# Second mixture of experts: results are scattered with addition onto stored features, and one array is read back

## The chip, the cores and the metric

The kernel runs on one core of a Trainium2 chip. Five engines matter: TensorE (PE in the profile, with its weight loads as PEld), VectorE (DVE), ScalarE (ACT), GpSimd (POOL) and SyncE (SP), which here only issues transfers. Each has its own instruction queue and waits on semaphores for the others. Sixteen DMA engines move data between the on-chip memory and the device memory; they take transfers from queues that SP, ACT and POOL fill. The metric is device time in microseconds (us) of one execution.

## The reference

The program is a net of four layers on a graph of N = 2708 nodes with D = 256 features, all in 32-bit floats. Each layer adds to the features x what a graph attention gives, and then what a feed-forward part gives. The change lies in the feed-forward part of layer 2, a decoder block with a mixture of experts:

```
x    = x + attention(rmsnorm(x)) @ wo.T          # causal, 4 heads
flat = rmsnorm(x)
probs = softmax(flat @ router_w.T)               # 8 experts
tp, ti = top_k(probs, 2)
tp   = tp / (sum(tp) + 1e-9)                     # the two shares of a node
weights = sum(tp[..., None] * one_hot(ti, 8))
for e in range(8):
    hh  = silu(flat @ w1[e].T) * (flat @ w3[e].T)    # 682 hidden units
    out = out + weights[:, e] * (hh @ w2[e].T)
x    = x + out
```

So each node's result is its own x, after attention, plus two weighted expert results. Layer 3 begins by normalizing that x and projecting it for its graph attention.

## The kernel before, in words

The features x stay on chip in an array X of 22 tiles of 128 nodes (the last has 20). `net_kernel` (L2406) runs the layers in order; `decoder_ffn` (L1486) is layer 2's feed-forward part and `elu_gnn` (L2368) layer 3's attention.

**Attention (L1878).** Nodes go in chunks of 512 (five, and a rest of 148). For each chunk `send` (L2052) multiplies by wo on PE, adds to X on POOL (L2066), forms the normalized row h and the logits of the eight experts, and then runs `Routing.chunk` (L1632). The order of PE is written out by hand: the score and value products run in groups of two steps, and between them one piece of the generator `sends`, up to its next `yield`, is let in (two pieces a group in the last column). The last chunk's `send` runs inside the mixture. On the other engines a planner sets the order by the data's dependences and by the `issue_after` marks.

**Routing (`Routing`, L1556).** `chunk` finds each node's two best experts, counts nodes per expert, ranks each node within its expert by two small PE products (L1661, L1662), and so gives each of its two choices a slot. Per tile of nodes, two indirect transfers on POOL (L1682) scatter the rows of h to the array hs in device memory, which is ordered by slots. A row carries 256 features and two tags (L1680): the node's number and the slot of its first choice.

**Mixture (`experts`, L2184).** `through` (L2266) runs over 47 slot tiles of 128 rows, each of one expert. For a tile it loads f from hs, transposes it (`front`), multiplies by w1 and w3 (`hidden`, L2226), applies silu on ACT, multiplies on DVE (`gate`, L2243), transposes again (L2250, copied to ht by DVE at L2251 and ACT at L2252), multiplies by w2 (`results`, L2258) and copies y out of PSUM on ACT (L2262). There are three buffers of y and two of hh, whose padding POOL clears (L2237). `where` (L1818) finds each row's target with three small DVE operations, and `send` (L1831) scatters y by an indirect transfer on POOL (L1834) to `ys`, which has one block of rows for first choices, one for second choices, and spare rows for empty slots. All targets are distinct, which line L1841 declares, so a send waits for no other send.

The queue of SP carries the loads of the weights: w2 early, w1 (L1552) from 1829.5 us, w3 from 1890.7 us, then the loads of f.

**Weights and end.** After the last slot tile's silu and gate, `shares` (L1501, called at L2355) computes the softmax over all logits and the two shares of every node, for all tiles together. `combine` (L1846) then reads both blocks of `ys` back, on the queues of SP, POOL and ACT, and `gat_single` (L1301), layer 3's attention, draws on it chunk by chunk: four tiles get their eight weighted additions on DVE (L1872), then the norm (L160 to L167, L124), the transposes (L1346) and projections on PE. Layer 1's top-1 mixture uses the same class with one choice: one array, one addition a tile. After the reads, the graph's mask is loaded again (L2452).

Of the kernel before, what the change touches and what calls it, by code (L numbers as in the profile page):

```python
# [8 lines left out]
F32 = mybir.dt.float32  # L9
# [3 lines left out]
ALU = mybir.AluOpType  # L13
# [1472 lines left out]
def decoder_ffn(net, ctx):  # L1486

    nc, tc, a = net.nc, net.tc, net.a  # L1490
    big = ctx.enter_context(tc.tile_pool(name="d_big", bufs=1))
    dram = ctx.enter_context(tc.tile_pool(name="d_dram", bufs=1, space=bass.MemoryType.DRAM))
    route = Routing(net, big, dram, 2, "d")
    ln2 = net.load_rows(big, a["d_ln2"], D, "ln2")
    router = net.load_weight(big, a["d_routerT"], "router")
    prep = ctx.enter_context(tc.tile_pool(name="g3prep", bufs=1))
    with ExitStack() as inner:
        weights = Weights(net, inner)
        heads = []

        def shares(work):  # L1501

            route.weights(work)
            total = work.tile([P, NT], F32, name="total")
            nc.vector.tensor_tensor(total, route.weight[:, 0, :], route.weight[:, 1, :], ALU.add)
            nc.vector.tensor_scalar(total, total, 1e-9, None, ALU.add)
            nc.vector.reciprocal(total, total)
            for c in range(2):
                nc.vector.tensor_tensor(route.weight[:, c, :], route.weight[:, c, :], total, ALU.mult)

        def head(work=None):

            if work is None:
                for _ in heads[0].fold():
                    pass
            else:
                heads.append(Head(net, prep, work, "g3", False))

        def mixture(after, rest):
            experts(net, route, weights, after, rest, head, shares)  # L1520

        attention(net, route, ln2, router, weights, mixture)
    return heads[0], route
# [32 lines left out]
class Routing:  # L1556
# [10 lines left out]
    def __init__(self, net, pool, dram, choices, key):  # L1567
# [4 lines left out]
        if choices == 1:  # L1572

            self.hs = dram.tile([E * CAP, 1], F32, name=f"{key}nodes")
        self.ys = dram.tile([(choices * NT + self.tiles) * P, D], F32, name=f"{key}ys")
        self.logits = pool.tile([P, NT, E], F32, name=f"{key}logits")
# [3 lines left out]

        self.tag = pool.tile([P, NT, 2], F32, name=f"{key}tag")
        nc.gpsimd.iota(
# [19 lines left out]
        for t, pattern, base, step in (  # L1602
            (self.s, [[1, S]], -E, 0),
            (self.at, [[0, 1]], 0, 1),
            (self.place, [[P, S]], choices * NT * P, 1),
        ):
            nc.gpsimd.iota(t, pattern, base=base, channel_multiplier=step, allow_small_or_imprecise_dtypes=True)
# [4 lines left out]
        if choices == 1:  # L1612
            zero = pool.tile([P, E * CAP // P], F32, name=f"{key}zero")
            nc.vector.memset(zero, 0.0)
            nc.scalar.dma_start(self.hs.rearrange("(p c) d -> p (c d)", p=P), zero)
        self.expert = pool.tile([1, S], I32, name=f"{key}expert")
        self.further = pool.tile([1, 1], I32, name=f"{key}further")
# [14 lines left out]
    def chunk(self, work, psum, t0, n, source, tag="pr"):  # L1632
# [3 lines left out]
        key = self.key  # L1636
        rest = self.logits[:, t0 : t0 + n, :]
        for c in range(self.choices):
            one, _ = first_max(nc, work, rest, net.rev, (n, E), P, f"{key}f{c}")
            oc = self.one[:, c, t0 : t0 + n, :]  # L1640
# [16 lines left out]
        nc.vector.tensor_copy(self.count, so_far[:, n, :])  # L1657
        yield
        ps = psum.tile([P, n, E], F32, name="rank", tag=tag)
        flat = ps.rearrange("p n e -> p (n e)")  # L1660
# [13 lines left out]
        for k in range(n):  # L1674
# [6 lines left out]
            for c in range(self.choices):  # L1681
# [7 lines left out]
                tc.declare_no_dep(i.ins, group=f"{key}scatter", reason="slots are distinct")  # L1689
                tc.add_to_no_dep_group(f"{key}scatter", i.ins)  # L1690

    def cut(self, psum, tag):
# [125 lines left out]
    def where(self, work, s, f, cut=False):  # L1818

        nc = self.net.nc  # L1820
        own, taken, spare = self.cuts if cut else (self.own, self.taken, self.spare)
        to = work.tile([P, 1], I32, name="to", bufs=8)
        at = work.tile([P, 1], F32, name="second", bufs=3)
        nc.vector.tensor_scalar(
            at, f[:, D + 1 :], own[:, s : s + 1], float(NT * P), ALU.not_equal, ALU.mult
        )
        nc.vector.tensor_scalar(at, at, f[:, D : D + 1], taken[:, s : s + 1], ALU.add, ALU.mult)
        nc.vector.tensor_tensor(to, at, spare[:, s : s + 1], ALU.add)
        return to

    def send(self, to, y):  # L1831
# [46 lines left out]
def attention(net, route, ln2, router, weights, mixture):  # L1878
# [11 lines left out]
    with ExitStack() as ctx:  # L1890
# [161 lines left out]
        def send(n, rp, aux, tag="aux"):  # L2052
# [6 lines left out]
            for k, t in enumerate(its):  # L2059
# [6 lines left out]
                nc.gpsimd.tensor_tensor(X[:r, t, :], X[:r, t, :], xa[:r], ALU.add)  # L2066
                h = hs[t] = rp.tile([P, D + 2], F32, name="h", bufs=len(its) + 1)
# [115 lines left out]

def experts(net, route, weights, after, rest, head, shares):  # L2184

# [6 lines left out]
    with ExitStack() as ctx:  # L2192
# [7 lines left out]
        def fetch(s, engine=None):  # L2200
            fs[s] = work.tile([P, D + 2], F32, name="f", bufs=E)
            route.load(s, fs[s], engine)
# [52 lines left out]
        def results(s, ht):  # L2255
# [5 lines left out]
            y = work.tile([P, D], F32, name="y", bufs=3)  # L2261
            nc.scalar.copy(y, po)  # L2262
            route.send(tos.pop(s), y)
            return last
# [65 lines left out]
        def routing():  # L2330
# [13 lines left out]
            with tc.issue_after(copied[-1].ins), tc.issue_after(route.sent.ins):  # L2344
                head(room)
            rooms.append(room)

        rooms, silus, gates, copied = [], [], [], []
        with tc.issue_after(after.ins):
# [56 lines left out]
def net_kernel(ctx, tc, a, out):  # L2406
# [3 lines left out]
    kept = dram.tile([N, N], U8, name="kept")  # L2410
    net.hs = dram.tile([Routing.E * CAP, D + 2], F32, name="hs")
    with ExitStack() as graph:
# [16 lines left out]
def clear_dispatch(net, pool):  # L2429

    nc = net.nc
    zero = pool.tile([P, D + 2], F32, name="zero")
    nc.gpsimd.memset(zero, 0.0)
    for e in range(Routing.E):
        nc.sync.dma_start(
            net.hs[e * CAP : (e + 1) * CAP].rearrange("(t p) d -> p t d", p=P),
            zero.unsqueeze(1).to_broadcast([P, NT, D + 2]),
        )
# [112 lines left out]
```

## Time and profile before

Three runs took 2600.6, 2603.6 and 2616.84 us. The table is of the profiled execution.

| what | value |
|---|---|
| median of the runs | 2603.6 us |
| the profiled execution's own time | 2609.1 us |
| its span | 2607.2 us |
| mean granted PE clock | 0.967 |
| attention of layer 2, last chunks | 1560 to 1895 us |
| PE's wait for the first f of the mixture | ends at 1904.96 us |
| last send of the mixture | 2301.21 us |
| first transpose of layer 3 | 2320.78 us |
| first attention product of layer 3 | 2366.31 us |

Times are read as microseconds from the start of the span. A line of a timeline gives the start, the duration, the engine, the line of the kernel, the operation with its output and inputs, the number of instructions put together, and in brackets how long the engine had been idle and what released it. A "q" after an engine's name is its instruction queue, in which it issues transfers.

### The profile page before, as it was taken

Reading aid. Unit: us, or ns where it says so; the run is one execution under the profiler, and the core shown is the slowest. Engines: PE = TensorE matmul, PEld = TensorE weight load, DVE = VectorE, ACT = ScalarE, POOL = GpSimd, SP = SyncE. Lnnn points to the kernel's source line nnn. Section 1 sums busy time; section 2 is a strip of 40 time slices with the busy share of each in tenths; the row PEclk is TensorE's granted clock in tenths of the full one; section 3 lists DMA queues with packets and bytes.
Section 4 is the critical chain, followed back from the end, with each engine's and each line's share of the span. In section 5 each row is a group of like instructions: output and inputs, shape, how many; then the busy total and the mean of one; then the engine's idle time right before and its main releaser. Section 6 shows DMA issues by size and latency. Waiting matters only on the chain. (4 is left out here: it accounts for less than half of the span.)

```text
span 2607.2 us, 32662 instructions
## 1 busy us (share of the span) xinstructions
PE 2422.9 (93%) x11708; PEld 1574.6 (60%) x11708; DVE 1477.6 (57%) x3288; ACT 1051.7 (40%) x1692; POOL 336.2 (13%) x476
## 2 busy tenths in 40 slices
PE   5899998999999998979799989999979999969998
PEld 4666765685333334568588854444457777747886
DVE  7754437746888875333545458778742222264556
ACT  3444443214787762321444324344412222234454
POOL 1000003100000000144130011222321111110002
PEclk9999999979999999989899999999989999979999
DMA  8899611000000003774310010000341111050001
GB/s 289 285 291 317 200 57 62 1 6 1 1 1 1 1 1 103 174 186 136 96 58 1 1 39 9 19 17 17 113 142 33 33 33 33 19 206 6 1 1 43
DMA packets 106859, 197.58 MB, mean 76 GB/s; under 512 B 8862, under 2 KB 63752, under 8 KB 103860
## 3 DMA queue, kind: packets, MB, share of 16 engines
q1 hardware_dynamic: 88010, 146.82, 18.2%
q0 software_dynamic: 14880, 43.76, 5.2%
q10 hardware_dynamic: 3806, 4.85, 0.6%
q8 instruction: 99, 1.62, 0.3%
q14 instruction: 64, 0.52, 0.1%
HBM read 135.69 MB, written 59.71 MB: 75 GB/s over the span
## 5 line engine op out<-in xcount | busy, mean ns | idle before, releaser
L732 DVE SCALAR_TENSOR_TENSOR e<-e,mask 128x768 f32<-128x768 f32 (+3 forms) x352 | 417.5, 1217 | 242.0 <-ACT e L731 239.4
L731 ACT ACTIVATE e<-big_p,minus_one,ratio 128x768 f32<-128x768 f32 (+3 forms) x352 | 418.6, 1226 | 281.3 <-PE acc L1463 193.4
L1463 PE MATMUL acc<-V,e 128*128 128x257 f32 x1848 | 401.9, 380 | 5.7 <-DVE e L732 5.6
L1463 PEld LDWEIGHTS acc<-V,e 128*128 128x128 f32 x1848 | 350.3, 190 | 57.5 <-issue 7.0
L2226 PE MATMUL h<-w,ft 128*128 (+1 forms) x752 | 234.5, 453 | 0.5 <-ACT ft L2208 0.5
L307 PE MATMUL acc<-F,e 128*128 128x257 f32 (+1 forms) x924 | 212.5, 383 | 4.1 <-DVE e L303 3.8
L928 PE MATMUL acc<-e,V 128*64 128x512 f32 (+1 forms) x1056 | 208.6, 547 | 1.3 <-DVE e L732 1.3
L307 PEld LDWEIGHTS acc<-F,e 128*128 128x128 f32 (+1 forms) x924 | 171.6, 189 | 57.0 <-DVE e L303 29.6
L2243 DVE TENSOR_TENSOR hh<-hh,h 128x682 f32<-128x682 f32 x47 | 40.7, 866 | 243.6 <-PE h L2226 243.6
L2226 PEld LDWEIGHTS h<-w,ft 128*128 128x128 f32 x752 | 135.9, 191 | 56.5 <-issue 1.8
L928 PEld LDWEIGHTS acc<-e,V 128*64 128x64 f32 x1056 | 73.6, 137 | 150.7 <-issue 145.6
L2014 ACT ACTIVATE e<-sc 128x1024 f32<-128x1024 f32 (+4 forms) x131 | 107.5, 863 | 137.5 <-PE sc L2005 97.8
L303 DVE TENSOR_TENSOR e<-e,mask 128x512 f32<-128x512 f32 (+2 forms) x132 | 80.5, 621 | 140.4 <-ACT e L296 138.7
L2036 DVE TENSOR_TENSOR sum<-sum,e 128x1024 f32<-128x1024 f32 (+4 forms) x131 | 137.1, 1047 | 20.6 <-PE po L2030 7.4
L296 ACT ACTIVATE e<-score 128x512 f32<-128x512 f32 (+2 forms) x132 | 69.4, 544 | 171.0 <-PE score L294 145.9
L2258 PE MATMUL po<-w,ht 114*128 (+1 forms) x564 | 131.5, 383 | 0.9 <-DVE ht L2251 0.9
L2005 PE MATMUL sc<-qt,kt 64*128 64x512 f32 (+5 forms) x568 | 121.0, 544 | 1.1 <-ACT sum L2014 0.9
L2258 PEld LDWEIGHTS po<-w,ht 114*128 114x128 f32 x564 | 107.6, 191 | 23.1 <-DVE ht L2251 8.2
L939 PE MATMUL den<-e,low 128*3 128x512 f32 (+1 forms) x1056 | 117.7, 542 | 0.0
L294 PE MATMUL score<-QK 128*128 128x512 f32 (+2 forms) x264 | 112.1, 553 | 3.4 <-ACT e L296 3.0
L2030 PE MATMUL po<-e,V 128*64 128x512 f32 (+5 forms) x524 | 108.5, 531 | 1.9 <-DVE e L2020 1.5
L2252 ACT COPY ht<-pt 114x256 f32<-114x256 f32 x47 | 17.5, 372 | 200.7 <-DVE ht L2251 200.7
(647 smaller groups left out, 3381.1 us busy)
## 6 DMA issues: line engine op xcount, KB each, us to landing
row<-in_adj SPq DMA_DIRECT2D x21, 1354.0 KB
raw<-in_adjT SPq DMA_DIRECT2D x35, 768.0 KB
hs<-zero SPq DMA_DIRECT2D x8, 2838.0 KB
hidden<-hr SPq DMA_DIRECT2D x32, 256.0 KB
wd<-in_f_wd SPq DMA_DIRECT2D x8, 1024.0 KB
kept<-mask SPq DMA_DIRECT2D x21, 338.5 KB
mask<-kept SPq DMA_DIRECT2D x21, 338.5 KB
w<-in_d_w1T SPq DMA_DIRECT2D x8, 682.0 KB
```

Source lines behind the costliest of these rows:

```text
L294: nc.tensor.matmul(ps[:r, :iw], QK[:, 0, span(j)], QK[:, 1, i0 : i0 + iw], start=True, stop=True)
L307: ended = nc.tensor.matmul(acc[k], e[:r, k * P : (k + 1) * P], F[:r, j, :], start=j == 0, stop=j == NT - 1)
L731: nc.scalar.activation(v, big_p[:, i], AF.Relu, bias=net.minus_one, scale=ratio)
L732: return nc.vector.scalar_tensor_tensor(v, v, 1.0, net.mask[:, j, i], ALU.add, ALU.mult)
L928: nc.tensor.matmul(acc[n][half, :iw], V[:, j, h, :], e[n][:, k, :iw], start=j == 0, stop=j == NT - 1)
L939: nc.tensor.matmul(den[g : g + Q, :iw], low[:, j, h, Q - 1 - q : 2 * Q - 1 - q], e[n][:, k, :iw], start=False, stop=j == NT - 1 and q == Q ...
L1463: nc.tensor.matmul(acc[k][:ri], e[:, k * P : k * P + ri], V[:, j, :], start=j == 0, stop=j == NT - 1)
L2005: nc.tensor.matmul(by_pairs(ps[:r, g], m, iw)[:, :, o:], kt[b, span(j)], qt[b, :, o:iw], start=True, stop=True)
L2030: nc.tensor.matmul(by_pairs(outs[n, p][b], m, iw)[:, :, o:], V[:r, j, g, :], by_pairs(e[:r, g], m, iw)[:, :, o:], start=j == 0, stop=j == ...
L2036: nc.vector.tensor_tensor(total, total, by_heads(e[:r], m, iw)[:, :, :, o:], ALU.add)
L2226: last = nc.tensor.matmul(halves[s, n][:, q, :HALF], fts[s][:, c, :], weights.w13[n][:, es[s], c, q * HALF : (q + 1) * HALF], start=c == 0 ...
L2258: last = nc.tensor.matmul(po, ht[:KP, k, :], w2[:KP, es[s], k, :], start=k == 0, stop=k == KC - 1)
```

## The change

For the mixture with two choices:

- `chunk` computes the shares of its nodes itself (the new `Routing.shares`: ten DVE operations and one Exp on ACT for each chunk, and one more `yield`). They travel as two more tags with h, so that a row of hs has 260 floats and not 258. The softmax after the last slot tile is gone.
- `send` of the attention stores the new X of its chunk to `ys` (`keep`, seven transfers on SP's queue in all). `ys` has one block of node rows, and one block of spare rows that is zeroed at the start.
- `where` takes four small DVE operations: one for the target, three for the row's own share. The copy of y on ACT multiplies by that share.
- The scatter of y adds to what its target row holds (`compute_op` add). Two sends can have rows in common, so the declaration that they are independent is left out, and a send waits for the one before.
- `combine` reads the one array straight into X by nine transfers on SP's queue. The weighted additions on DVE are gone.
- `left` does for slot tiles beyond the usual 47 what `where` had done with a bigger spare block; it runs only if there are such tiles.

The mixture with one choice keeps its path, with a tag array of four columns.

```diff
@@ Routing.__init__
-        self.ys = dram.tile([(choices * NT + self.tiles) * P, D], F32, name=f"{key}ys")
+        spare = self.tiles if choices == 1 else 1
+        self.ys = dram.tile([(NT + spare) * P, D], F32, name=f"{key}ys")
...
-        self.tag = pool.tile([P, NT, 2], F32, name=f"{key}tag")
+        self.tag = pool.tile([P, NT, 4], F32, name=f"{key}tag")
...
+        else:
+            zero = pool.tile([P, D], F32, name=f"{key}zero")
+            nc.vector.memset(zero, 0.0)
+            nc.scalar.dma_start(self.ys[NT * P :, :], zero)
@@ Routing.chunk
         nc.vector.tensor_copy(self.count, so_far[:, n, :])
         yield
+        if self.choices == 2:
+            self.shares(work, t0, n, *most)
+            yield
         ps = psum.tile([P, n, E], F32, name="rank", tag=tag)
@@ new in Routing
+    def shares(self, work, t0, n, top, second):
+        nc, E, key = self.net.nc, self.E, self.key
+        e = work.tile([P, n, E + 1], F32, name=f"{key}e")
+        nc.vector.tensor_tensor(
+            e[:, :, :E], self.logits[:, t0 : t0 + n, :], top.unsqueeze(2).to_broadcast([P, n, E]), ALU.subtract
+        )
+        nc.vector.tensor_tensor(e[:, :, E], second, top, ALU.subtract)
+        nc.scalar.activation(e, e, AF.Exp)
+        w0, w1 = self.tag[:, t0 : t0 + n, 2], self.tag[:, t0 : t0 + n, 3]
+        nc.vector.tensor_reduce(w0, e[:, :, :E], AX.X, ALU.add)
+        nc.vector.reciprocal(w0, w0)
+        nc.vector.tensor_tensor(w1, e[:, :, E], w0, ALU.mult)
+        total = work.tile([P, n], F32, name=f"{key}sum")
+        nc.vector.scalar_tensor_tensor(total, w0, 1e-9, w1, ALU.add, ALU.add)
+        nc.vector.reciprocal(total, total)
+        for w in (w0, w1):
+            nc.vector.tensor_tensor(w, w, total, ALU.mult)
+
+    def keep(self, its):
+        for k0, k1, r in whole_and_rest(its):
+            r0 = its[k0] * P
+            self.net.nc.sync.dma_start(
+                self.ys[r0 : r0 + (k1 - k0 - 1) * P + r, :].rearrange("(t p) d -> p t d", p=r),
+                self.net.X[:r, its[k0] : its[k0] + k1 - k0, :],
+            )
@@ Routing.where
         to = work.tile([P, 1], I32, name="to", bufs=8)
-        at = work.tile([P, 1], F32, name="second", bufs=3)
-        nc.vector.tensor_scalar(
-            at, f[:, D + 1 :], own[:, s : s + 1], float(NT * P), ALU.not_equal, ALU.mult
-        )
-        nc.vector.tensor_scalar(at, at, f[:, D : D + 1], taken[:, s : s + 1], ALU.add, ALU.mult)
-        nc.vector.tensor_tensor(to, at, spare[:, s : s + 1], ALU.add)
-        return to
+        w = work.tile([P, 2], F32, name="share", bufs=8)
+        slot = f[:, D + 1 : D + 2]
+        nc.vector.scalar_tensor_tensor(to, f[:, D : D + 1], taken, spare, ALU.mult, ALU.add)
+        nc.vector.tensor_scalar(w[:, 1:], slot, own, f[:, D + 3 :], ALU.not_equal, ALU.mult)
+        nc.vector.tensor_scalar(w[:, :1], slot, own, f[:, D + 2 : D + 3], ALU.is_equal, ALU.mult)
+        nc.vector.tensor_tensor(w[:, :1], w[:, :1], w[:, 1:], ALU.add)
+        return to, w[:, :1]
@@ Routing.send
             in_offset=None,
+            **({} if self.choices == 1 else {"compute_op": ALU.add}),
         )
-        tc.declare_no_dep(i.ins, group=f"{self.key}results", reason="rows are distinct")
-        tc.add_to_no_dep_group(f"{self.key}results", i.ins)
+        if self.choices == 1:
+            tc.declare_no_dep(i.ins, group=f"{self.key}results", reason="rows are distinct")
+            tc.add_to_no_dep_group(f"{self.key}results", i.ins)
@@ Routing.combine
+        if self.choices == 2:
+            for t0, t1 in ((0, 1), (1, 2), (2, 4), (4, 8), (8, 12), (12, 16), (16, 20), (20, NT)):
+                for k0, k1, r in whole_and_rest(range(t0, t1)):
+                    r0 = (t0 + k0) * P
+                    self.read = nc.sync.dma_start(
+                        X[:r, t0 + k0 : t0 + k1, :],
+                        self.ys[r0 : r0 + (k1 - k0 - 1) * P + r, :].rearrange("(t p) d -> p t d", p=r),
+                    )
+            yield
+            return
@@ attention.send
+            route.keep(its)
             for k, t in enumerate(its):
@@ experts.results
             y = work.tile([P, D], F32, name="y", bufs=3)
-            nc.scalar.copy(y, po)
-            route.send(tos.pop(s), y)
+            to, share = tos.pop(s)
+            nc.scalar.activation(y, po, AF.Copy, scale=share)
+            route.send(to, y)
@@ experts, end
-        with tc.issue_after(silus[-1].ins), tc.issue_after(gates[-1].ins):
-            shares(rooms[0])
         with route.others():
+            route.left()
             through(0, E)
             through(route.usual, route.tiles)
```

More of the change, by code (lines that the diff above doesn't have):

```diff
@@ L1499, in decoder_ffn @@
         heads = []
[L1501 to L1509, printed above, removed]
         def head(work=None):
@@ L1519, in mixture @@
         def mixture(after, rest):
-            experts(net, route, weights, after, rest, head, shares)
+            experts(net, route, weights, after, rest, head)
         attention(net, route, ln2, router, weights, mixture)
@@ L1604, in __init__ @@
             (self.at, [[0, 1]], 0, 1),
-            (self.place, [[P, S]], choices * NT * P, 1),
+            (self.place, [[P if choices == 1 else 0, S]], NT * P, 1),
         ):
@@ L1636, in chunk @@
         key = self.key
-        rest = self.logits[:, t0 : t0 + n, :]
+        rest, most = self.logits[:, t0 : t0 + n, :], []
         for c in range(self.choices):
-            one, _ = first_max(nc, work, rest, net.rev, (n, E), P, f"{key}f{c}")
+            one, top = first_max(nc, work, rest, net.rev, (n, E), P, f"{key}f{c}")
+            most.append(top)
             oc = self.one[:, c, t0 : t0 + n, :]
@@ L1690, in chunk, with left @@
                 tc.add_to_no_dep_group(f"{key}scatter", i.ins)
+    def shares(self, work, t0, n, top, second):
[22 more added lines that the diff above has]
+            )
+    def left(self):
+        nc, E, (_, done, _) = self.net.nc, self.E, self.cuts
+        taken, spare, place = self.taken[:, :E], self.spare[:, :E], self.place[:, :E]
+        nc.vector.tensor_tensor(taken, taken, done, ALU.subtract)
+        nc.vector.tensor_tensor(spare, taken, place, ALU.mult)
+        nc.vector.tensor_tensor(spare, place, spare, ALU.subtract)
     def cut(self, psum, tag):
@@ L1820, in where @@
         nc = self.net.nc
-        own, taken, spare = self.cuts if cut else (self.own, self.taken, self.spare)
+        own, taken, spare = (t[:, s : s + 1] for t in (self.cuts if cut else (self.own, self.taken, self.spare)))
         to = work.tile([P, 1], I32, name="to", bufs=8)
-        at = work.tile([P, 1], F32, name="second", bufs=3)
-        nc.vector.tensor_scalar(
-            at, f[:, D + 1 :], own[:, s : s + 1], float(NT * P), ALU.not_equal, ALU.mult
-        )
-        nc.vector.tensor_scalar(at, at, f[:, D : D + 1], taken[:, s : s + 1], ALU.add, ALU.mult)
-        nc.vector.tensor_tensor(to, at, spare[:, s : s + 1], ALU.add)
-        return to
+        w = work.tile([P, 2], F32, name="share", bufs=8)
[5 more added lines that the diff above has]
+        return to, w[:, :1]
     def send(self, to, y):
@@ L2066, in send @@
                 nc.gpsimd.tensor_tensor(X[:r, t, :], X[:r, t, :], xa[:r], ALU.add)
-                h = hs[t] = rp.tile([P, D + 2], F32, name="h", bufs=len(its) + 1)
+                h = hs[t] = rp.tile([P, D + 4], F32, name="h", bufs=len(its) + 1)
                 nc.scalar.activation(h[:r, :D], xa[:r], AF.Square, accum_out=ss[:r, k : k + 1])
@@ L2181, in whole_and_rest, with experts @@
     return [(0, n, P)] + [(k, k + 1, rows(its[k])) for k in range(n, len(its))]
-def experts(net, route, weights, after, rest, head, shares):
+def experts(net, route, weights, after, rest, head):
     nc, tc = net.nc, net.tc
@@ L2200, in fetch @@
         def fetch(s, engine=None):
-            fs[s] = work.tile([P, D + 2], F32, name="f", bufs=E)
+            fs[s] = work.tile([P, D + 4], F32, name="f", bufs=E)
             route.load(s, fs[s], engine)
@@ L2345, in routing @@
                 head(room)
-            rooms.append(room)
-        rooms, silus, gates, copied = [], [], [], []
+        silus, gates, copied = [], [], []
         with tc.issue_after(after.ins):
@@ L2410, in net_kernel @@
     kept = dram.tile([N, N], U8, name="kept")
-    net.hs = dram.tile([Routing.E * CAP, D + 2], F32, name="hs")
+    net.hs = dram.tile([Routing.E * CAP, D + 4], F32, name="hs")
     with ExitStack() as graph:
@@ L2431, in clear_dispatch @@
     nc = net.nc
-    zero = pool.tile([P, D + 2], F32, name="zero")
+    zero = pool.tile([P, D + 4], F32, name="zero")
     nc.gpsimd.memset(zero, 0.0)
@@ L2436, in clear_dispatch @@
             net.hs[e * CAP : (e + 1) * CAP].rearrange("(t p) d -> p t d", p=P),
-            zero.unsqueeze(1).to_broadcast([P, NT, D + 2]),
+            zero.unsqueeze(1).to_broadcast([P, NT, D + 4]),
         )
```

## The prediction, made before the changed kernel was run

> **What bounds the kernel now.** First the busy table of the page, for the engine that carries the time. In every fence below a number after an x is a count, and a figure in brackets is idle time of the engine just before, with what ended it.
>
> ```profile
> PE 2422.9 (93%) x11708; PEld 1574.6 (60%) x11708; DVE 1477.6 (57%) x3288; ACT 1051.7 (40%) x1692; POOL 336.2 (13%) x476
> ```
>
> TensorE (PE) is busy 93% of the span, so an edit on DVE, POOL or a DMA queue counts only where PE waits for it. Second, the windows of the stages that the change touches: second attention, passage into the mixture, mixture, passage to the next layer. The columns are start:end and length, then busy time of PE, PEld, DVE, ACT and POOL, the granted PE clock, the DMA share and GB/s.
>
> ```profile
> 1560.00:1850.00 290.00, 282.41 (x1314) 120.91 (x1316) 230.50 (x467) 118.05 (x167) 66.33 (x61) 0.99 0.11 39
> 1850.00:1900.00 50.00, 36.49 (x230) 19.52 (x229) 35.12 (x97) 16.80 (x34) 14.57 (x17) 0.90 0.21 75
> 1950.00:2300.00 350.00, 347.86 (x1529) 255.61 (x1528) 96.94 (x235) 75.55 (x170) 46.16 (x85) 1.00 0.11 32
> 2300.00:2312.00 12.00, 0.53 (x3) 0.12 (x1) 0.40 (x4) 1.86 (x3) 6.02 (x9) 0.64 0.37 116
> 2312.00:2345.00 33.00, 21.71 (x83) 16.07 (x84) 32.48 (x110) 15.46 (x65) 3.32 (x4) 0.77 0.99 354
> ```
>
> Attention and mixture are PE bound (97% and 99%). PE stands still in two places: the passage in (13.5 of 50 us) and the passage out. There, from 2312 on, DVE is full (32.5 of 33 us) and so is the DMA (0.99). Third, the timeline of the passage out, for what follows what (start, duration, engine, line):
>
> ```profile
> 2301.21 0.97 POOL L1834 DMA_INDIRECT dys<-y,to  x1 [8.62 <-ACT y L2262]
> ...
> 2306.64 11.69 SPq L1860 DMA_DIRECT2D y<-dys  x7
> ...
> 2311.95 3.26 DVE L1872 SCALAR_TENSOR_TENSOR X<-y,dweight,X 128x256 f32<-128x256 f32 x8 [9.27 <-DMA y<-dys]
> ...
> 2316.87 3.23 DVE L1872 SCALAR_TENSOR_TENSOR X<-y,dweight,X 128x256 f32<-128x256 f32 x8
> 2316.99 0.30 ACT L163 ACTIVATE sd<-mv,ln_eps 128x4 f32<-128x4 f32 x1 [13.72 <-DVE mv L161]
> 2320.01 0.17 DVE L167 RECIPROCAL rstd<-sd 128x4 f32<-128x4 f32 x1
> ...
> 2320.78 1.51 PE L1346 MATMUL tp<-ident,f 128*128 128x128 f32 x6 [20.25 <-DVE f L124]
> ```
>
> The last send starts at 2301.21; its landing releases the reads 5.4 us later; they deliver 5.3 us later; eight weighted additions (3.26 us) precede the norm of the first four tiles, eight more (3.23 us) fall between the square root and its reciprocal; PE starts after 20.25 us of idleness. Fourth, the passage in, and one steady period of the mixture:
>
> ```profile
> 1880.96 0.99 POOL L1682 DMA_INDIRECT hs<-h,dto  x1 [14.61 <-DVE h L1680]
> 1904.96 0.66 PE L132 MATMUL tp<-ident,f 128*128 128x128 f32 x2 [14.07 <-DMA f<-hs]
> 2103.65 0.98 POOL L1834 DMA_INDIRECT dys<-y,to  x1 [4.26 <-ACT ft L2208]
> 2106.92 0.16 DVE L1828 TENSOR_TENSOR to<-second,dspare 128x1 int32<-128x1 f32 x1
> 2107.42 0.69 DVE L2251 COPY ht<-pt 114x512 f32<-114x512 f32 x1 [0.34 <-PE pt L2250]
> 2111.81 0.98 POOL L1834 DMA_INDIRECT dys<-y,to  x1 [4.26 <-ACT ft L2208]
> ```
>
> PE's 14.07 us wait at the entry is the routing of node chunk 4 (DVE), eight scatters of h, their landing, the load of f. In the mixture sends leave every 8.15 us.
>
> **The change, part by part.** The sums are against the profiled execution: span 2607.2 us, its own time 2609.1, which is 5.5 us above the median of 2603.6; a saving is carried to the median as it stands.
>
> *Passage out.* Removed: 44 weighted additions of about 0.41 us (3.26/8) and half of the reads (two arrays of 2.77 MB become one, read into X on SP's queue alone). Step by step: (1) The last landing. The bytes of a plain send have moved about 2 us after its start (the DMA share in the middle of the mixture peaks from 1.4 to 1.9 us after 2111.81), but the waiter is released at 5.4 us here, and at 2.5 us after the last send of layer 1's mixture (1253.89, reads issued 1256.43). No row shows an adding send. It also reads each row before it writes it. Nothing can make it shorter than a plain one, which the same writes already need, but its release could fall near layer 1's 2.5 us; at worst the read costs what a small read costs (a 129 KB load of f in mid-run: issue 2123.32, bytes in by 2125, 1.7 us) plus a second write-like burst, +2.8. I take +1.5, nearer the read's row: 2301.21 + 5.4 + 1.5 = 2308.1. Here the Trainium skill helps with one term: "Collectives: The Full Stack", section "The bandwidth ceiling: the fold count and why AG ≠ RS ≠ AR", says that an add needs two source reads and so half a copy's rate. On the 0.5 us burst that is +0.5 alone; I stay at 1.5, since the trace's own landing is 3 us longer than its burst. (2) Tiles 0 to 3 arrive. Before, 1 MB took 5.3 us; half of it at the window's 354 GB/s saves 1.5 us: 3.8. From the f load's 1.7 us and 384 KB more at that rate: 2.8. I take 3.4: 2311.5. (3) With no additions, what remains is the statistics of the last two tiles to arrive (0.74 + 0.18 us), square root 0.30, reciprocal to first transpose 0.77 (2320.01 to 2320.78): 2.1 with gaps. PE starts at 2313.6 instead of 2320.78: **−7.2**. (4) The first block of four tiles took 11.35 us (2320.78 to 2332.1) against 6.5 for later ones, DVE and clock both being behind; layer 1's passage, with half the additions, took 10.35. I take −1.5, bounds 0 and −4. After that PE is the bound. Total **−8.7**, from −5 (landing +2.8, delivery 3.8) to −14 (landing 2.5 to 4).
>
> *The end softmax* (some 5 us of DVE, an Exp and its table load of 1.28 us) lay at 2291 to 2299 beside the last results on PE, before the last send: removing it is 0.
>
> *Weights by chunk.* Per chunk ten small DVE operations and an Exp. A small DVE row here is 0.16 to 0.27 us; with a pitch of 0.21, 2.1 us a chunk. Chunks 0 to 3 fall into the attention, where DVE has 59 us free of 290 but its additions are one step from PE's tail work; PE is what is full, and cover holds except where PE waits for the rank or an X tile. 0 to 8.4 us; I take +0.5, by the 97%. Chunk 4 stands in the entry chain: +2.1 for DVE, an Exp that may queue behind one of 1.22 us on ACT, and the rank matmuls come a group later in PE's written order: +0.5 to +5, taken **+2.5**. The last chunk's Exp falls into the mixture and swaps ACT's table twice (2.56 us) in gaps of over 4 us: 0, at worst +2.6.
>
> *Storing X.* Seven writes (2.77 MB) on SP behind POOL's X additions, ahead of w1 and w3 and, for the last rows, of the f loads. The first would be queued by about 1830, when w1 went out at 1829.5 before; w1 is first needed at 1906, w3 shares the wire with the f loads: 2.77 MB at 400 GB/s is 7 us over 340 us. 0; if a late X addition holds SP, w1 moves and has 70 us of slack. POOL's first send now waits for all seven and for the zero fill: the last is out some 10 us before the first y.
>
> *In the loop.* Four small DVE operations for three per slot tile (47 tiles). DVE idles 0.34 us before the copy of ht, which PE waits for; one more row of 0.16 to 0.25 fits. If not, 47 × 0.2 = +9. Evicting y with a scale: 0.47 us (the 128x256 scaled copy on ACT elsewhere in this trace) for 0.37, with over 4 us idle before: 0, and +0.1 at the end.
>
> *The chain of sends.* The plain sends of one array were independent. Now each waits on POOL for the landing of the one before. Queued behind a waiting send on POOL is the memset of a later hh (L2237), for which DVE's gate and then PE wait; ACT waits when the three y buffers are full. By the rows a landing takes 5.4 + 1.5 = 6.9 us of the 8.15: 1.25 to spare, no cost. The rule that speaks against the change is in "DMA: Bandwidth & Descriptors", section "Rules for kernel authors": an adding DMA beside another access of the same bytes loses writes, so the earlier semaphore must be waited for; hence the chain is required. Its fit in "Anatomy of one DMA — SWDGE (gpsimd) path" (2.0 us and the bytes at 436 GB/s) would make an adding send 2.3 to 2.6 us, with 5.5 to spare and an end 4 us earlier. The trace's 5.4 decides.
>
> Sum: −8.7 + 2.5 + 0.5 = −5.7: profiled 2603.4, median **2598** (2603.6 − 5.7). About 1% (26 us) is what a measurement of this kernel can tell from no change, and the whole idle time at the passage out is 20 us.
>
> **The rivals.**
> A, the forecast, 2592 to 2610: 0.61.
> B, a larger gain: the last landing is seen after 2.5 us, the chunk-4 chain hides its ten operations, and the first block runs at the full clock. The landing saves another 4.4 (6.9 − 2.5), the block 4 in place of 1.5, the entry costs 0: −7.2 −4.4 −4 gives about 2588. For it: layer 1's landing. Against it: this mixture's own 5.4. 0.14.
> C, the loss ahead of the mixture: X additions, rank and Exp in the hand-written order hold PE in each chunk, +5 at the entry and 2 in each of four chunks, with the fourth operation of the loop hit: −8.7 + 13 + 6 gives about 2614. For it: DVE 80% full. Against: PE 97% busy there. 0.11.
> D, the other side: the chain of sends becomes the bound. It decides when start to landing of an adding send passes 8.15 us, the period. A send of 128 rows is 8 rows for each of 16 engines. If an engine finishes one row's read and write before the next, at about 0.8 us a row (an estimate, from the least HBM round trip on "DMA: Bandwidth & Descriptors", section "Latency and other measured facts"; no run here shows it), it is 2.5 + 6.4 = 8.9 us, and the y buffers hand the excess to PE: 46 × 0.75 = 35, about 2633; from the base of 5.4 it would be above 2700. For it: a margin of only 1.25 us. Against: a plain send's rows overlap (0.5 us burst), and nothing says that adding stops that. 0.14.
>
> **How the numbers follow.** A's 2592 to 2610 is wide by landing, delivery and entry. The range 2585 to 2622 takes in A, most of B and C, and leaves out D and the edges, under 2 in 10. Faster by over 1% (below 2577.6) needs all of the 20 us and more: 0.04. Slower by over 1% (above 2629.6) is most of D: 0.13. Else 0.83.
>
> **What would show it.** In the profile after: sends at a period of 8.15 us, POOL's idle time before them ended by a DMA landing but not lengthening; last send to first read of X about 7 us; no additions in the passage out, PE idle there about 13 us; f at the entry 2 to 3 us later; the mixture's window still 99% PE. Wrong would make it: a period above 8.15 (D), PE waits for rank or X in the attention (C), a landing of 2 to 4 us (B).

## The result, and the profile after

The changed kernel takes 2596.8 us (median of 20 runs, 2589.8 to 2603.3) against 2605.5 us for the kernel before beside it (20 runs, 2600.6 to 2616.8). The ratio is 0.9961, with a 95% interval of 0.9949 to 0.9973: 0.4% faster, some 10 us (7 to 13). The profiled execution has a span of 2595.1 us, 12.1 us less than before.

The busy table of the page of the changed kernel:

```profile
PE 2422.7 (93%) x11708; PEld 1576.9 (61%) x11708; DVE 1464.5 (56%) x3331; ACT 1058.4 (41%) x1698; POOL 358.2 (14%) x470
```

PE does the same work in the same busy time (2422.7 for 2422.9 us), so all that was won is PE's idle time. The windows of the changed kernel, with the columns of before (length, busy time of PE, PEld, DVE, ACT and POOL, granted clock, DMA share, GB/s):

```profile
1560.00:1850.00 290.00, 283.78 (x1326) 121.01 (x1326) 231.40 (x504) 119.17 (x172) 63.50 (x59) 1.00 0.13 44
1850.00:1900.00 50.00, 35.66 (x222) 19.29 (x220) 35.14 (x106) 16.30 (x33) 17.60 (x22) 0.87 0.30 105
1950.00:2300.00 350.00, 346.00 (x1528) 254.22 (x1526) 97.17 (x262) 79.12 (x170) 72.40 (x86) 1.00 0.21 33
2300.00:2312.00 12.00, 1.81 (x8) 1.47 (x8) 5.00 (x22) 1.57 (x7) 5.72 (x7) 0.50 0.69 197
2312.00:2345.00 33.00, 31.23 (x135) 23.07 (x136) 19.00 (x81) 23.03 (x104) 0.00 (x0) 0.97 0.68 252
2301.42:2334.42 33.00, 22.85 (x95) 16.98 (x96) 22.12 (x97) 17.48 (x74) 5.49 (x6) 0.81 0.91 322
```

The row from 2312 on can't be held against the same row of before: layer 3's first transpose comes 10.6 us earlier now, so the window shows a later part of the work. The last row is moved by those 10.6 us, and so stands at the same distance from that transpose as the window of before. There DVE, full before (32.5 of 33 us), is busy for 22.1, the DMA share falls from 0.99 to 0.91, and PE is busy for 22.9 us where it was 21.7. The timeline of the passage out, from the last send to the first transpose of layer 3:

```profile
2298.69 1.54 POOL L1869 DMA_INDIRECT dys<-y,to  x1 [6.34 <-ACT y L2311]
...
2303.78 5.06 SPq L1892 DMA_DIRECT2D X<-dys  x9
...
2305.98 0.43 DVE L160 BATCH_NORM_STATS2 bnst<-X 128x6 f32<-128x256 f32 x1 [4.01 <-DMA X<-dys]
...
2308.07 0.75 DVE L160 BATCH_NORM_STATS2 bnst<-X 128x6 f32<-128x256 f32 x2 [0.89 <-DMA X<-dys]
...
2309.08 0.30 ACT L163 ACTIVATE sd<-mv,ln_eps 128x4 f32<-128x4 f32 x1 [7.40 <-DVE mv L161]
...
2310.19 1.73 PE L1346 MATMUL tp<-ident,f 128*128 128x128 f32 x7 [12.28 <-DVE f L124]
```

From the last send to that transpose it is 11.5 us, where it was 19.6. No DVE row but statistics and norm is left in between, and the reciprocal (L167) follows its square root at once.

The profiles differ ahead of all this: the first score product of layer 2 starts anywhere between 1531 and 1543 us in the profiles of this study, with nothing changed in front of it. So stages are compared from that product (S) on. F is the first transpose of the mixture (it needs the first f), T the first transpose of layer 3, A its first attention product. Times in us, differences of starts:

| profile | S to F | F to first send | sends 1 to 46 | send 46 to 47 | send 47 to first read | send 47 to T | send 47 to A | S to A |
|---|---|---|---|---|---|---|---|---|
| before | 366.5 | 16.9 | 369.7 | 9.6 | 5.4 | 19.6 | 65.1 | 827.9 |
| changed | 364.7 | 17.2 | 369.0 | 7.9 | 5.1 | 11.5 | 53.7 | 812.5 |
| b_chain | 366.6 | 16.3 | 369.7 | 9.6 | 5.7 | 19.9 | 64.1 | 826.2 |
| a_plain | 364.6 | 17.3 | 369.0 | 7.9 | 3.6 | 10.5 | 53.3 | 812.0 |
| a_adds | 363.2 | 16.2 | 369.0 | 9.6 | 5.0 | 17.0 | 61.2 | 819.2 |
| a_reads | 364.4 | 17.4 | 369.0 | 7.9 | 5.2 | 12.9 | 57.2 | 815.8 |
| a_shares2 | 364.4 | 17.4 | 369.0 | 7.9 | 4.9 | 10.9 | 53.5 | 812.2 |
| b_yield | 362.9 | 16.2 | 369.2 | 9.6 | 4.6 | 18.6 | 62.7 | 820.7 |
| a_noyield | 368.7 | 17.5 | 369.4 | 7.9 | 5.0 | 11.0 | 53.4 | 817.0 |
| a_end | 364.5 | 17.3 | 369.0 | 7.9 | 5.5 | 11.7 | 53.9 | 812.6 |
| a_split | 364.7 | 17.2 | 369.0 | 7.9 | 5.0 | 11.1 | 53.5 | 812.4 |
| a_yield2 | 359.5 | 16.4 | 369.5 | 9.6 | 5.1 | 11.7 | 54.1 | 809.0 |
| a_yield3 | 374.4 | 16.3 | 369.5 | 9.6 | 5.0 | 11.6 | 54.0 | 823.8 |

The last send is send 47. Each row is one profile of one execution; profiles of kernels that do the same in a stage differ there by up to 1.5 us from S to F and 2.4 us from send 47 to A.

In these two profiles the changed kernel gains 15.4 us from S to A: 11.4 behind the last send, 1.7 in the last slot tile, 1.8 ahead of the mixture. From A to the end it took 1.8 us more than before (242.7 for 240.9; b_chain, whose PE order there is that of before, took 242.4), and S itself came 1.5 us later.

### The profile page after: what moved, and what is told of

It reads as the page before. It is cut to its first block, busy times and chain, and to the rows that moved or that the text cites. A ratio compares the mean times of both kernels' runs of the same rounds, so it can differ in the third digit from the quotient of the medians.

```text
span 2595.1 us, 32725 instructions
## 1 busy us (share of the span) xinstructions
PE 2422.7 (93%) x11708; PEld 1576.9 (61%) x11708; DVE 1464.5 (56%) x3331; ACT 1058.4 (41%) x1698; POOL 358.2 (14%) x470
## 5 line engine op out<-in xcount | busy, mean ns | idle before, releaser
L1869 POOL DMA_INDIRECT dys<-y,to x47 | 73.7, 1569 | 208.1 <-ACT ft L2256 190.8
```

## The experiments

The theory to begin with: the gain is the passage out, from the additions that DVE no longer makes and, for a smaller part, from half the reads; the chain of sends and the end softmax are covered by PE. The rivals: the chain costs something at each slot tile; the reads are the gain; and for the 1.8 us ahead of the mixture, where a loss of 3 us had been forecast, either another order of PE's work or something outside it. Each ratio is to the kernel before, with its 95% interval.

### The chain alone, and the addition alone

b_chain, from the kernel before:

```diff
-        tc.declare_no_dep(i.ins, group=f"{self.key}results", reason="rows are distinct")
-        tc.add_to_no_dep_group(f"{self.key}results", i.ins)
+        if self.choices == 1:
+            tc.declare_no_dep(i.ins, group=f"{self.key}results", reason="rows are distinct")
+            tc.add_to_no_dep_group(f"{self.key}results", i.ins)
```

> The kernel before, with the declaration that its sends are independent left out, so that each plain send waits for the landing of the one before; nothing else changes. Theory (the chain has room): the start-to-landing of about 5 us fits in the period of 8.15 us, so the time is that of before within 0.15% (4 us), sends at 8.15 us. Rival (the chain costs something at every slot tile): 46 periods longer by 0.2 us or more, +9 us and up. Also a second look at the last product of the mixture: before it took 4.51 us at a granted clock of 0.66, after 2.83 us; if the end softmax causes the slow clock, it is slow here too.

Measured: 0.9998 (0.9988 to 1.0008). The chain costs nothing. Because each send is now waited for by the next, the trace can say how long one takes to land. The line for the sends of 1930 to 2200 us:

```profile
L1834 POOL DMA_INDIRECT dys<-y,to x33: 976/979/1031, 1937.1 to 2195.9; - x33
...
DMA to landing us min/median/max: 2.4/2.4/3.9
```

a_plain, from the changed kernel:

```diff
-            **({} if self.choices == 1 else {"compute_op": ALU.add}),
```

> The changed kernel with a plain store in place of the addition (it leaves out the sum of X and the two results: a later row replaces the earlier one). Everything else, the chain of waits too, stays. Theory (the addition is free): POOL's instruction falls from 1.56 to about 0.97 us, the last landing by 0 to 0.6 us, total within 0.1% (3 us) of the changed kernel. Rival (the addition makes the landing longer): last send to first read falls from 5.1 us to 3.6 or less, total 1.5 us or more lower.

Measured: 0.9949 (0.9930 to 0.9967), against 0.9961 for the changed kernel: not told apart. The profile tells them apart: the first read comes 3.6 us after the last send and not 5.1. In the changed kernel the line for the sends of 1930 to 2200 us is:

```profile
L1869 POOL DMA_INDIRECT dys<-y,to x33: 1547/1566/1669, 1931.2 to 2192.9; - x33
...
DMA to landing us min/median/max: 3.6/3.8/3.9
```

So an adding send of 128 rows of 1 KB lands after 3.8 us and a plain one after 2.4: the addition costs 1.4 us, and POOL's own instruction 1.57 us for 0.98. What the engines do is seen in windows of half a microsecond behind the send of 2111.34 us in the changed kernel:

```profile
2113.00:2113.50 0.50, 0.50 (x4) 0.30 (x3) 0.32 (x1) 0.00 (x0) 0.00 (x0) 1.00 0.16 6
2113.50:2114.00 0.50, 0.50 (x3) 0.17 (x1) 0.50 (x2) 0.00 (x0) 0.00 (x0) 1.00 1.05 80
2114.00:2114.50 0.50, 0.50 (x5) 0.40 (x5) 0.50 (x4) 0.00 (x0) 0.00 (x0) 1.00 0.96 150
2114.50:2115.00 0.50, 0.50 (x6) 0.50 (x5) 0.20 (x2) 0.00 (x0) 0.00 (x0) 1.00 0.20 27
```

The same for the kernel before, behind its send of 2103.65 us:

```profile
2105.15:2105.65 0.50, 0.50 (x4) 0.30 (x3) 0.06 (x1) 0.00 (x0) 0.00 (x0) 1.00 0.72 262
```

The share is a mean over the 16 engines. An adding send keeps it full for about 1 us, at 80 to 150 GB/s; a plain one is over within this half microsecond, at 262 GB/s. Added up over the rows, an adding send takes 1.2 us of all engines and a plain one 0.36, about a third. So the theory that the addition is free did not hold for the landing. In the passage out of the changed kernel and of a_plain a further 1.2 us lie between the landing (3.9 and 2.4 us there) and the first read.

In the kernel before the first read came only 5.4 us after the last send, though that send is plain as well. The trace shows what held it: 1.58 us after the send started, one transfer of 16 KB on a queue that the profile calls "instruction" began, and it lasted 1.45 us. The last three packets of the send went out only as that transfer ended, and the send's bytes were all moved at 3.71 us after its start, where the sends of 2103.65 and of a_plain's end needed 2.06. In b_chain such a transfer ended at 3.42 us and the send at 3.44; in b_yield, below, at 2.19 and 2.89. In a_plain it began at 2.76, behind the send. The view of the DMA queues from 2.1 to 3.8 us after the last send has these rows, in the kernel before (three packets of the send are still to come) and in a_plain (none is):

```profile
q0 software_dynamic: 3, 0.01, 2.6%
```

```profile
q8 instruction: 1, 0.02, 4.2%
```

This accounts for 1.65 of the 1.8 us by which the first read of before is later than a_plain's. In b_chain it accounts for 1.4 of 2.1; the rest of that is open. The 3.9 us at the end of b_chain's line of landings above is another send that met such a transfer.

### How much room the chain has

a_twice, from the changed kernel:

```diff
             route.send(to, y)
+            route.send(to, y)
```

> The changed kernel with every send of y issued twice, one after the other (each result is added twice, so the sums differ). Two landings must then fit in a period. Theory (an adding send takes 3.8 us to land, so about 4.0 to 4.4 us from start to the start of the next with the wait): two take 8.0 to 8.8 us, so the chain is just about the bound, period 8.2 to 8.8 us, +0 to +30 us on the changed kernel. Rival (the landing in the mixture is what the passage out shows, 5.1 us): period 10.2 us, +95 us. Rival (a fixed 2.3 to 2.6 us each): no change, period 8.15 us.

Measured: 1.0086 (1.0064 to 1.0107), 2631.1 us, +34 us on the changed kernel's 2596.8. The timeline of POOL in the mixture of a_twice, with one row of PE's weight loads:

```profile
2108.09 1.54 POOL L1869 DMA_INDIRECT dys<-y,to  x1 [2.45 <-DMA dys<-y,to]
2109.07 0.68 POOL L2285 MEMSET hh<- 128x2 f32 x1
...
2109.80 0.13 PEld L2298 LDWEIGHTS pt<-ident,hh 128*114 128x114 f32 x1 [0.31 <-POOL hh L2285]
...
2112.91 1.56 POOL L1869 DMA_INDIRECT dys<-y,to  x1 [3.16 <-DMA dys<-y,to]
2116.97 1.54 POOL L1869 DMA_INDIRECT dys<-y,to  x1 [2.50 <-DMA dys<-y,to]
2117.95 0.68 POOL L2285 MEMSET hh<- 128x2 f32 x1
2122.05 1.56 POOL L1869 DMA_INDIRECT dys<-y,to  x1 [3.42 <-DMA dys<-y,to]
```

Now every send waits for a landing. From the first send (1916.46) to the first send of the last pair (2322.89) it is 406.4 us, 8.84 a pair in the mean, and 46 × (8.84 − 8.15) = 32 us. One adding send occupies the chain for 4.0 us when the next stands ready (the send of 2108.09 began 2.45 us after the end of the one before it, which had taken 1.56; from 2112.91 to 2116.97 it is 4.06). The other send of a pair follows after 4.8 to 5.1 us; what the difference is made of was not found. PE feels the chain by the way that the prediction named: POOL clears the padding of hh behind a waiting send, and PE's weight load then waits for that clearing, for 0.31 us at 2109.80. The changed kernel therefore has about 4 of its 8.15 us to spare, and two sends a tile are just too many: the end of the theory's own interval, slightly passed. The 5.1 us of the passage out are not the price of a send in the chain.

### Additions and reads, each put back

a_adds, from the changed kernel:

```diff
+            for n0, nw in chunks(512):
+                for t in tiles_of(n0, nw):
+                    r = rows(t)
+                    for c in range(2):
+                        last = nc.vector.scalar_tensor_tensor(
+                            X[:r, t, :], X[:r, t, :], self.weight[:r, c, t : t + 1], X[:r, t, :], ALU.mult, ALU.add
+                        )
+                yield last
-            yield
             return
```

> The changed kernel with 44 additions of 128x256 on DVE put back where before had them (X times zero plus X, two a tile, after the reads). Theory (the additions are what the passage out saves): 8 x 0.41 = 3.3 us before the first statistics and 3.2 us before the reciprocal, so the first transpose comes 6.5 us later, and some 2 us more are lost over the first blocks: +6 to +9 us on the changed kernel, about 2602 to 2605. Rival (the saving is in the reads): +3 us or less.

a_reads, from the changed kernel (n is the chunk of t0, its the chunk's tiles):

```diff
+                if t0 % 4 == 0:
+                    y = pool.tile([P, 4, D], F32, name="y1", bufs=len(chunks(512)))
+                    engine = nc.scalar if n == 0 else queues[(n + 1) % 2]
+                    for k0, k1, r in whole_and_rest(its):
+                        engine.dma_start(y[:r, k0:k1, :], ...)
```

> The changed kernel with a second read of the one array, into tiles that nothing uses, on the queues that carried the second array before. Theory (the reads are the smaller part): tiles 0 to 3 arrive 1 to 2 us later, total +1 to +3 us on the changed kernel. Rival (the traffic is the saving): +6 us or more, with the DMA share back at 0.99 from 2312 to 2345 us and the first blocks waiting for X.

Measured: a_adds 0.9975 (0.9965 to 0.9985), a_reads 0.9973 (0.9963 to 0.9984), each slower than the changed kernel's 0.9961 by about 3 us. The intervals overlap, so the times alone say little; the stages say more. With the additions back, T comes 17.0 us after the last send, 5.5 us later than in the changed kernel, and A 7.4 later. With the reads back, T comes 1.4 us later and A 3.5. The timeline of a_adds has the pattern of before again, additions ahead of the statistics and ahead of the reciprocal:

```profile
2298.30 2.19 DVE L1902 SCALAR_TENSOR_TENSOR X<-X,dweight 128x256 f32<-128x256 f32 x5 [0.75 <-DMA X<-dys]
...
2302.16 3.22 DVE L1902 SCALAR_TENSOR_TENSOR X<-X,dweight 128x256 f32<-128x256 f32 x8
2302.28 0.30 ACT L163 ACTIVATE sd<-mv,ln_eps 128x4 f32<-128x4 f32 x1 [11.25 <-DVE mv L161]
2305.30 0.17 DVE L167 RECIPROCAL rstd<-sd 128x4 f32<-128x4 f32 x1
...
2306.06 1.73 PE L1346 MATMUL tp<-ident,f 128*128 128x128 f32 x7 [17.77 <-DVE f L124]
```

Held at the same distance from the last send as the moved window above, a_adds has DVE busy for 31.7 of 33 us at a DMA share of 0.79, and a_reads has DVE at 22.2 and a share of 0.96. In the window that its rival named (2312 to 2345 us) a_reads has a share of 0.78, and not 0.99.

Together 7.4 + 3.5 = 10.9 us, against 11.4 that the passage lost from before to after. By these profiles the additions are about two thirds of it and the reads about one third; with kernels like the one before taking 62.7 to 65.1 us from the last send to A, the split is rough. In time a_adds lost about 3.6 us on the changed kernel, less than the 6 to 9 expected.

### The end softmax, and the slow last product

a_end, from the changed kernel:

```diff
+        with tc.issue_after(silus[-1].ins), tc.issue_after(gates[-1].ins):
+            p, m, total = route.logits, route.tag[:, :, 3], route.tag[:, :, 2]
+            ...
+            nc.scalar.activation(p, p, AF.Exp)
+            ...
+            for c in range(2):
+                nc.vector.tensor_tensor(route.weight[:, c, :], route.weight[:, c, :], total, ALU.mult)
         with route.others():
             route.left()
```

> The changed kernel with the end softmax put back after the last gate (the same thirteen DVE operations and one Exp, in place on tiles that nothing needs any more). Theory (it is covered): the time of the changed kernel within 0.1% (3 us), the last send and the passage out as there. Rival (it caused the slow last product of before): the last 12 products take 4.5 us again, +1.7 us. Second rival (it delayed the reads of before, 5.4 us after the last send where a plain send after the change needs 3.6): the first read comes 6 us or more after the last send.

Measured: 0.9961 (0.9942 to 0.9981), equal to the changed kernel, as is its profile: last product 2.83 us, T 11.7 us after the last send. The softmax was covered. The last 12 products, which took 4.51 us at a granted clock of 0.66 before, take 4.51 in a_adds, which has no end softmax, and 2.83 in a_end, which has it:

```profile
2283.78 4.51 PE L2315 MATMUL po<-w,ht 114*128 x12 [0.88 <-DVE ht L2308]
```

So the 1.7 us between sends 46 and 47 do not belong to the softmax. In the table they go with the time from F to the first send: 16.2 to 16.9 us with the slow last product, 17.2 to 17.5 without it. In the slow ones the granted clock is 0.5 for 3.4 us, from 4.6 to 5.0 us before the last send on, in the kernel before, a_adds and a_yield2; in the changed kernel, a_end and a_noyield it does not fall there. Why it falls in the one case and not in the other was not found.

### The order of PE's work ahead of the mixture

PE's waits in the attention, with who ended them and how long (total, count, longest). Shown are waits for the routing, and those that change most. Before:

```profile
PE wy L139 <- DVE yt L2049: 3.2, 1, 3.2
PE rank L1661 <- DVE dtaken L1652: 2.2, 1, 2.2
PE pj L1976 <- DVE drank L1664: 2.0, 1, 2.0
```

and in the changed kernel:

```profile
PE wy L139 <- DVE yt L2096: 1.8, 1, 1.8
PE rank L1660 <- DVE dtaken L1648: 1.0, 1, 1.0
PE sc L2052 <- ACT sum L2061: 0.9, 1, 0.9
PE pj L2023 <- DVE xa L2112: 0.9, 1, 0.9
```

Ten DVE operations a chunk more, and PE waits less. The added `yield` lets the tail of a chunk come one group later, when DVE has more of it ready. Five runs try this. a_shares2, from the changed kernel:

```diff
             self.shares(work, t0, n, *most)
+            self.shares(work, t0, n, *most)
             yield
```

> The changed kernel with the per-chunk shares computed twice (ten more DVE operations and one more Exp a chunk). Theory (they lie beside PE's work and beside DVE's own waits): the stage from the first score product to the first f of the mixture stays at 364.7 us within 0.7 us. Rival (they stand in the entry chain, as the prediction had it): +2 to +3 us in that stage, all between chunk 4's logits and the first scatter.

b_yield, from the kernel before:

```diff
         nc.vector.tensor_copy(self.count, so_far[:, n, :])
         yield
+        if self.choices == 2:
+            yield
```

> The kernel before with one more empty yield in the routing of a chunk, where the changed kernel has one; no arithmetic is moved. Theory (the gain of 1.8 us in the attention is PE's written order: what follows the ranks of a chunk comes one group later, and PE's waits for the ranks, for yt and for the projection shrink): the stage from first score product to first f goes from 366.5 to about 364.7 us. Rival (the gain comes from elsewhere, such as the w1 loads or the clock): it stays at 366.5 us.

a_noyield, from the changed kernel:

```diff
             self.shares(work, t0, n, *most)
-            yield
```

> The changed kernel without the yield after the shares, so that PE's written order has the ranks as early as before. Theory (order): the stage goes back up to 366.5 us or above, with PE waiting over 2.2 us for the rank, since the shares now also stand ahead of it. Rival: it stays at 364.7 us.

a_yield2 has one `yield` more than the changed kernel at that place, a_yield3 two.

> The changed kernel with one more empty yield after the shares. Theory (the first yield gained by moving the tail work of a chunk one group later, past PE's waits): a second one gains less, 0 to 2 us in the stage from first score product to first f, since the wait for the rank is only 1.0 us now. Rival (later is worse at the end of the last column): the last scatter of chunk 4 comes later, +1 to +4 us.

> The changed kernel with two more empty yields after the shares. Theory (each yield gains by what PE still waits for, and the second one left only 0.2 us for ranks and 0.4 us for xa): the stage from first score product to first f stays at about 359.5 us, or turns back up by 1 to 4 us because the tail of a chunk ends later. Rival (later is better without end): -4 us or more again, about 355 us.

Measured, as ratio and as stage from S to F: a_shares2 0.9960 (0.9943 to 0.9977), 364.4 us; b_yield 1.0001 (0.9984 to 1.0018), 362.9; a_noyield 0.9965 (0.9954 to 0.9976), 368.7; a_yield2 0.9950 (0.9931 to 0.9970), 359.5; a_yield3 1.0000 (0.9988 to 1.0012), 374.4.

The waits follow the order. In b_yield, which computes no shares, they are those of the changed kernel:

```profile
PE wy L139 <- DVE yt L2051: 1.9, 1, 1.9
PE rank L1663 <- DVE dtaken L1652: 1.0, 1, 1.0
```

In a_noyield, which computes them, they are close to those of before:

```profile
PE wy L139 <- DVE yt L2095: 2.7, 1, 2.7
PE rank L1659 <- DVE dtaken L1648: 2.2, 1, 2.2
```

Doubling the shares costs nothing in the stage. Taking the `yield` away costs 4.0 us, and then the changed kernel is 2.2 us behind the kernel before; giving the kernel before that `yield` saves 3.7. So the gain is the order, and the shares with all else that the change brings there cost about 2. A second `yield` saves another 5.2 us: the waits for yt are gone from PE's list, and 0.2 us are left for the ranks. A third loses 15, in the stage and in the time: PE now waits elsewhere, as the list of a_yield3 shows.

```profile
PE sc L2054 <- ACT e L2063: 4.4, 2, 4.2
PE tp L1998 <- DVE dlogits L2148: 2.6, 1, 2.6
PE pj L2025 <- DVE xa L2114: 1.6, 2, 0.9
```

Those waits are 9 of the 15 us. Chunk 4's last logits come 13 us later than in a_yield2; what makes up the other 6 us was not traced. Both expectations missed the size: 0 to 2 us of gain for the second `yield`, 1 to 4 us of loss for the third. Of the times, only a_yield3's is clearly away from the changed kernel's; the smaller steps are read from single profiles, and b_yield's gain of 3.7 us is hidden in an interval of 4.4 us to either side.

### Reads on two queues

a_split, from the changed kernel:

```diff
-            for t0, t1 in ((0, 1), (1, 2), (2, 4), (4, 8), ...
+            for t0, t1 in ((0, 1), (1, 2), (2, 3), (3, 4), (4, 8), ...
-                    self.read = nc.sync.dma_start(
+                    self.read = (nc.scalar if t0 in (1, 3) else nc.sync).dma_start(
```

> The changed kernel with the first four tiles of X read one by one, tiles 0 and 2 on SP's queue, 1 and 3 on ACT's. Theory (the delivery of 4.3 us is issue and wire one after the other on one queue): tile 3 arrives 1 to 1.5 us earlier and the first transpose with it, total -1 us. Rival (the delivery is the wire): no change of the first transpose, 11.5 us after the last send.

Measured: 0.9969 (0.9957 to 0.9982), not told apart from the changed kernel. T comes 11.1 us after the last send for 11.5, 0.4 us, less than the profiles of like kernels differ by (10.9 to 11.7), so no gain is shown.

The best version of the study is a_yield2 (2590.2 us, 0.9950), which beats the kernel before clearly, and the changed kernel by 3.5 us from S to A; in time the two are not told apart.

## Why the prediction was right, and where it was not

It forecast 2598 us, a gain of 5.7; measured are 2596.8 us and a ratio worth 10 (7 to 13). The direction and the reason hold, the sum is short, and one of its terms has the wrong sign. That 2598 lies so near 2596.8 is luck in part: the kernel before took 2605.5 us beside the changed one, 1.9 more than the three runs that the forecast started from. The gain itself was nearly twice the forecast. Of rival B two signs came true in part: the last landing was shorter than forecast, and chunk 4's operations cost nothing to be seen at the entry.

**Passage out, −8.7.** Shown by a_adds and a_reads, and mis-sized: 11.4. From the last send to T the forecast was −7.2 and 8.1 were measured. Its terms: the landing and release was put at 6.9 us (5.4 and 1.5) and took 5.1. The price of the addition was near (1.4 measured for 1.5), though it was picked between bounds of 0 and 2.8. The base was not: the 5.4 us of before are not what a plain send needs in that place, which is 3.6 (a_plain). The prediction took the 2 us in which a send's bytes move from the middle of the mixture and so put the rest of the 5.4 us down to the landing. At the last send of before the bytes themselves took 3.7 us, since a 16 KB instruction transfer stood in the way of the last packets. The delivery was put at 3.4 and took 4.3 (2303.78 to 2308.07), the norm at 2.1 and took 2.1. From T to A the forecast was −1.5; 45.5 us became 42.2, −3.3, of which b_chain (44.2) lets 1.3 be chance.

**Weights by chunk, +0.5 and +2.5.** This step failed in the changed kernel as it is: −1.8 instead of +3.0. The price itself was about right, since without the `yield` the stage is 2.2 us longer than before, though the doubled shares cost nothing, so that the 2.2 us can't be laid to the DVE operations. The step named the later rank matmuls as a cost. They were a gain, for PE stood waiting there for DVE in the profile of before, in the waits of 2.2 and 3.2 us that the windows' 97% hid.

**The loop and the chain of sends, 0.** Right: sends at 8.15 us, b_chain equal to before, the fourth small DVE operation under its cover. The working was not: the room was put at 1.25 us, from the passage out's 5.4 us, and is about 4. The fit of the Trainium skill ("DMA: Bandwidth & Descriptors", section "Anatomy of one DMA — SWDGE (gpsimd) path"), 2.3 us for these bytes, was the nearer figure for a plain send in the mixture (2.4), and the adding one at 3.8 lies between that and the 6.9 taken. Rival D, the chain as the bound, therefore needed twice the sends to come true (a_twice).

**End softmax, storing X, eviction, 0.** The first is shown by a_end. For the others no run stands alone; w1 went out at 1827.6 us and f arrived when it had before.

Outside the sum lie the 1.7 us of the last slot tile. They were no part of the forecast and go with the granted clock; a_adds, a_yield2 and a_yield3, which have the change, lack them. Whether the change has a part in when the clock falls is not shown.

## What to carry to other kernels

An accumulating scatter moves an addition away from a busy engine, and its chain cost nothing here, where a landing of 3.8 us fits into a period of 8.15: measure the landing in the steady loop, not at one place at the end, where the release of the next stage is counted with it and another transfer may stand in its way. Compare windows at the same distance from an event, not at the same time. A generator's `yield` in an order written by hand is an edit of the schedule: look at the list of PE's waits, not at its busy share, to say which way it goes, and try one more or one less. Putting the additions back delayed the first transpose by 5.5 us and the first attention product by 7.4: what leaves a passage also moves the next blocks' work forward.

## What the runs showed of the hardware

- An indirect send of 128 rows of 1 KB lands in 2.4 us when it stores and in 3.8 when it adds; POOL's instruction takes 0.98 and 1.57 us. The adding one takes 1.2 us of all DMA engines, the plain one 0.36.
- Adding sends that wait for one another follow at 4.0 us when the next stands ready; a pair took 8.8 us in a_twice.
- One 16 KB transfer of the instruction queue, 1.45 us long, held the last packets of a plain send until 3.7 us after its start, for 2.06 without it (before; also b_chain and b_yield).
- From a landing to the first transfer that SP issues behind it, it was 1.2 us (a_plain, 2.4 to 3.6; the changed kernel, 3.9 to 5.1).
- The 12 last products of the mixture took 2.83 or 4.51 us, at a granted clock of 1.00 or 0.66, in kernels that do the same there.
